# A two-layer graph network on one core: the second layer's first product from quarters, a norm in its input's place, and channel sums turned by VectorE

## The chip, the cores and the metric

The kernel runs on one core of a Trainium2 chip. A core has five engines that run side by side and wait for each other through semaphores: TensorE (PE in the profile) for matrix products, VectorE (DVE), ScalarE (ACT), GpSimd (POOL) and SyncE (SP), which here only starts transfers. The engines work on SBUF, an on-chip memory of 128 partitions; matrix products land in PSUM, a smaller memory in banks of 512 floats a partition. Each engine carries out its instructions strictly in the order in which the program lists them. The metric is the time of one execution on the device in microseconds.

## The reference

Sixteen graphs share one weighted adjacency matrix `adj` of 1024 nodes; every node carries 256 channels. All is in 32-bit floats. Two layers follow each other, each with a residual connection:

```python
h = relu(layernorm(x))
# layer 1, for each graph: attention whose queries come from a reweighted graph
c   = mean over channels of h                       # one number per node
A   = 2 * abs(abs(sigmoid(c_j - c_i) - 0.5) - 0.5)  # node by node
q   = relu((h^T @ (adj * A)) * para)^T
k,v = split(h @ kv_w)
x   = x + softmax(q k^T * scale) v                  # 4 heads of 64 channels
h = relu(layernorm(x))
# layer 2: aggregation over the normalised graph, and two linear layers
agg = A_hat @ h                                     # A_hat from adj + I and its degrees
y   = agg @ W1^T + b1                               # 256 -> 512 channels
out = relu(batchnorm(y)) @ W2^T + b2                # 512 -> 256 channels
x   = x + batchnorm(out)
```

The batch norms take their mean and variance over all nodes of all 16 graphs, so y is kept in memory (HBM) until all graphs are through, and read again.

## The kernel before

**The frame.** `attention` walks over all graphs in steps. A graph has four units (two head pairs by two halves of the queries) of four steps, 16 steps a graph. A step issues the scores of two blocks of keys (`scores`, L933), their exponentials p on ACT (L941), the running sum `acc` of p on VectorE (L962, L965) and the product with v of the step before (`Unit.values`, L976). After a unit's last step follow, at fixed later steps, a fold of acc (L1011, L1012), the softmax sums (L1025 to L1039), the attention output turned by VectorE in squares of 32 (L990), stored and fetched back, and its addition to x (L1074, L1082).

Behind each step the program issues a share of other work, the "background": generators that yield a cost for each piece. `attention` takes pieces until their summed cost reaches what is due by this step; the dues follow from constants (`total`). So the order on every engine is fixed when the program is written out. A `weave` runs side generators along a main one, and `soon` puts an action behind the next piece.

**The background of graph b**, in this order: four pieces of keys of graph b+1 (`keys_values`), the queries of graph b+1 (`queries`: seven products in place of eight, from sums and differences of quarters), the values of graph b+1, along with them the norm of graph b-1 after its attention (`normed`), the aggregation of graph b-1 (`aggregate`, seven products again), along with it the first norm of graph b+2 (`summed`), and at last `hidden(b-1)`, the second layer's first product, along with which `prepare` turns h of graph b+2 by way of memory (`squares`, `gathered`) and starts the weights of its reweighted graph.

**hidden.** For each of two halves of the nodes (512 columns) and four blocks of 128 output channels, two products over the two halves of the 256 input channels are summed in one PSUM bank (`bank`, three of them in rotation); ACT adds the bias and copies the result to SBUF (L773), POOL starts its store (L774), and VectorE takes its statistics (L777). The function `product` splits each product into two of 64 output rows.

**The weights w.** `differences` stores the channel sums of a graph and reads them back as one row broadcast to all partitions, `cbc`. For each tile of w, `weigh` lets ACT take |c_j - c_i| twice (L485) and a tanh (L493), and VectorE multiplies with adj (L472). From graph 2 on the sums are stored in the order (partition, tile), so that L485 reads cbc with a step of eight floats; graphs 0 and 1 have them in node order.

**Buffers.** x of three graphs is held at a time (pool p3, tag "x"); h has two buffers (p2, tag "h") which the norms of both layers and the turned copy `sq` share; y has four.

Of the kernel before, what the change touches and what calls it, by code (L numbers as in the profile page):

```python
# [23 lines left out]
def gnn_two_layers_kernel(  # L24
# [34 lines left out]
    vec = const.tile([P, 18], F32, name="vec")  # L59
    nc.sync.dma_start(out=vec, in_=vecs)  # L60
    b1, g1, be1 = (vec[:, i * HC : (i + 1) * HC] for i in range(3))
    b2, g2, be2 = (vec[:, 3 * HC + i * CC : 3 * HC + (i + 1) * CC] for i in range(3))
# [34 lines left out]
    def layers(shifted):  # L97
# [13 lines left out]
        py = st.enter_context(tc.tile_pool(name=f"py_{kind}", bufs=4))  # L111
# [7 lines left out]

        xs, hs, hts, ats, qs, ks, vs = {}, {}, {}, {}, {}, {}, {}  # L120
        invs = {}
        csums, cbcs, weighted, weighers = {}, {}, {}, {}
# [5 lines left out]
        def soon(action):  # L128

            queue.append(action)  # L130
# [33 lines left out]
        def bank(name):  # L164
            return ps_mm.tile([P, FB], F32, tag="mm", name=name)
# [7 lines left out]
        def load_x(b):  # L173
            xs[b] = p3.tile([P, NT, C], F32, tag="x", name=f"x_{b}")
            parts = 4 if b == 0 else 2
            for part in range(parts):
                t = slice(part * NT // parts, (part + 1) * NT // parts)
                nc.sync.dma_start(
                    out=xs[b][:, t], in_=x[b].rearrange("(t p) c -> p t c", p=P)[:, t]
                )  # L180
# [108 lines left out]

        def load_later():  # L290
            later["w1"] = big.tile([P, CC, H1], F32, tag="w1", name="w1")
            nc.sync.dma_start(out=later["w1"], in_=w1_t.rearrange("(k p) j -> p k j", p=P))
            later["dbc"] = const.tile([P, N], F32, tag="dbc", name=f"dbc_{kind}")
            nc.sync.dma_start(out=dinv_d.rearrange("(t p) -> p t", p=P), in_=dinv)
            nc.sync.dma_start(
                out=later["dbc"], in_=dinv_d.rearrange("(o n) -> o n", o=1).to_broadcast([P, N])
            )

        class Norm:
# [3 lines left out]
            def __init__(self, b, first):  # L303
                tag = "a" if first else "b"
                self.src = xs[b]
                self.st6 = p1.tile([P, NT, 6], F32, tag="st6", name=f"st6_{tag}_{b}")
                self.mv = p1.tile([P, NT, 2], F32, tag="mv", name=f"mv_{tag}_{b}")
                self.sm = p2.tile([P, 3, NT], F32, tag="lnsm", name=f"lnsm_{tag}_{b}")
                self.csum = None
                if first:  # L310
                    self.csum = p2.tile([P, NT], F32, tag="csum", name=f"csum_{b}")
                    csums[b] = self.csum
                self.h = p2.tile([P, NT, C], F32, tag="h", name=f"h_{tag}_{b}")
                hs[tag, b] = self.h
# [113 lines left out]
        def differences(b):  # L428

            cbc = p1.tile([P, N], F32, tag="cbc", name=f"cbc_{b}")
            cbcs[b] = (
                cbc.rearrange("p (t q) -> p t q", t=NT)
                if b <= 1
                else cbc.rearrange("p (q t) -> p t q", t=NT)
            )
            weighers[b] = weigh(b)
            if b == 0:
                broadcast_row(cbc, columns_of(csums[b], f"c{b}"), f"c{b}")  # L440
                return
            if b == 1:
                turned = bank(f"csumt_{b}")[0:NT, 0:P]
                nc.tensor.transpose(turned, csums[b], ident)
                row = p1.tile([P, NT // 2, P], F32, tag="s1", name=f"csumr_{b}")[0:NT, 0, :]
                nc.scalar.copy(row, turned)
                nc.sync.dma_start(out=csum_d[b].rearrange("(t p) -> t p", p=P), in_=row)
            else:
                nc.sync.dma_start(out=csum_d[b].rearrange("(p t) -> p t", p=P), in_=csums[b])
            nc.sync.dma_start(  # L450
                out=cbc, in_=csum_d[b].rearrange("(o n) -> o n", o=1).to_broadcast([P, N])
            )
# [229 lines left out]
        def aggregate(b):  # L682
# [3 lines left out]
            order = (0, 2, 5, 1, 4, 6, 3)  # L686
# [35 lines left out]
            def sixth(m):  # L722
                add(c21, m, c21)
                soon(lambda: scale(c21, 0))
# [5 lines left out]
            for i, (left, after) in enumerate(  # L730
# [5 lines left out]
                    (None, fifth),  # L736
                    (a22, sixth),
                    (a12, seventh),
# [4 lines left out]
                for th in range(NP // 2):  # L743
# [7 lines left out]
                    if th == NP // 2 - 1:  # L751
                        after(made)
                    elif i == 0:
                        combine("b", b, nc.vector)
                    yield 1.71

        def hidden(b):

# [31 lines left out]
        def normed(b):  # L790
            while (b, NH - 1) not in complete:
                yield 0.1
            keep(b)
            yield from Norm(b, False).all()
            if b + 3 < B:
                load_x(b + 3)
# [15 lines left out]
        def prepare(b, products):  # L812
# [4 lines left out]
            if b == 2:  # L817
                for k in range(CC):
                    yield from weave(islice(products, 3), (0, islice(w, AHEAD // 2)))
                    yield TOP  # L820
                    transposed(b, (k,))
                    yield 1.0
                yield from products
                return
            squares(b)
            yield from weave(islice(products, 3), (0, islice(w, AHEAD // 2)))
            gathered(b, 0)
            yield from weave(islice(products, 1), (0, islice(w, 1)))
            gathered(b, 1)
            yield from weave(islice(products, 2), (0, islice(w, AHEAD // 2 - 1)))  # L830
# [4 lines left out]
        def background(b):  # L835

            if b == 0:
                differences(1)
                for k in range(CC):
# [3 lines left out]
                w, products, norm = weighers[1], keys_values(1), Norm(2, True).all()  # L843
                yield from weave(
                    islice(products, 4), (0, double(islice(w, 8))), (0, islice(norm, 4))
                )
                yield from weave(
                    plain_queries(1), (0, norm), (0, w), (5, graph()), (7, degrees())
                )
                differences(2)  # L850
                yield from islice(products, 2)
                yield from prepare(2, products)
# [3 lines left out]
            if b + 1 < B:  # L856
# [5 lines left out]
                yield next(gather)  # L862
                yield from weave(products, (0, norm))
            else:
                yield from weave(endings.pop(), (2, normed(b - 1)))
                yield next(gather)
# [225 lines left out]
        def attention():  # L1092
# [7 lines left out]
            for s in range(len(steps) + 2):  # L1100
                if s < len(steps):
                    unit, g = steps[s]
                    b = unit.at[0]
                    if s % per_graph == 0:
# [4 lines left out]
                        total += 13.7 * (0 < b < B - 2) + 27.4 * (b == B - 1) + 3.0 * (b == 0)  # L1109
# [20 lines left out]
                if before is not None:  # L1130
                    (last, g_last), prs = before
                    last.values(g_last, prs)
                    if g_last == NG - 1:
# [6 lines left out]
                        else:  # L1140
                            for e in range(2):
                                at_end.setdefault(s + e, []).append(lambda u=last, e=e: u.fold(e))
                            wait = 5 if last.by_squares and last.at[1:] == (0, 0) else 4
                            at_mid.setdefault(s + wait - 1, []).append(last.sums)
# [18 lines left out]
        with st:  # L1163
# [22 lines left out]
            else:  # L1186
# [24 lines left out]
                load_x(1)  # L1211
                load_x(2)
                run(weave(plain_queries(0), (0, weighers[0]), (5, Norm(1, True).all())))
                attention()
# [349 lines left out]
```

## Time and profile before

| | |
|---|---|
| median of 3 runs | 2489.23 us (2488.91 to 2490.34) |
| profiled execution | 2488.76 us, its span 2487.0 us |
| PE, DVE, ACT, POOL busy | 2435.7, 1882.0, 1401.7, 429.2 us |
| PE's granted clock | 0.993 of full speed |
| matmuls of hidden (`py`) | 1024 instructions, 228.4 us |
| w's activations (L485) | 256 of 1168 ns on average |
| copies of y (L773), statistics of y (L777) | 128 of 683 ns, 128 of 677 ns |
| moved by transfers | 421.42 MB, 169 GB/s on average |

How to read it: a row of the profile names the source line, engine, operation, the written and the read tile with their shapes, and the count; then the busy time in us and the mean of one in ns; then the time for which the engine stood idle just before these instructions and who ended the wait. A matmul in 32-bit floats shows as two PE instructions. Busy times of one row may overlap, since instructions are pipelined. L171 is the line of `product`, so its rows are told apart by the tiles' names: pg queries, pk keys, pv values, pa aggregation, py hidden. SPq and POOLq are the instructions that start transfers.

### The profile page before, as it was taken

The page shows a single profiled execution, that of the slowest core. Times are in us where ns is not written, and L with a number is a line of the kernel's source. Part 1 is how long each engine was busy: PE and PEld are TensorE (multiplying, and loading weights), DVE is VectorE, ACT ScalarE, POOL GpSimd, SP SyncE. Part 2 cuts the span into 40 slices and gives each one's busy share as a digit, 9 for nine tenths or more (in the row PEclk, how much of TensorE's full clock was granted, in tenths as well). Part 3 has the DMA queues.
Part 4 walks back from the last instruction along what each step waited for, and adds up shares of the span by engine and source line. Part 5 has one row for each costly group of instructions (what it writes and reads, how often), then busy time and mean ns, then how long its engine had stood idle before and what let it go on. Part 6 is the DMA issues. An engine that isn't in the chain of part 4 may idle for free. (4 is left out here: it accounts for less than half of the span.)

```text
span 2487.0 us, 35569 instructions
## 1 busy us (share of the span) xinstructions
PE 2435.7 (98%) x13403; PEld 841.2 (34%) x13403; DVE 1882.0 (76%) x2920; ACT 1401.7 (56%) x1927; POOL 429.2 (17%) x527
## 2 busy tenths in 40 slices
PE   9999999999999999999999999999999999999995
PEld 4333333333333333333333333333333332334444
DVE  5668787877778787878787787868787877767775
ACT  7775564647473746656474747465564634345544
POOL 1640101010101001011101010110101001036652
PEclk9999999999999999999999999999999999999997
DMA  4754535354545545362645445543536344355559
GB/s 150 238 173 172 170 114 199 101 199 129 197 145 178 164 159 169 116 206 84 215 126 182 145 174 169 178 153 132 191 94 210 116 140 162 132 214 220 189 199 374
DMA packets 187909, 421.42 MB, mean 169 GB/s; under 512 B 21832, under 2 KB 81744, under 8 KB 181968
## 3 DMA queue, kind: packets, MB, share of 16 engines
q1 hardware_dynamic: 158560, 311.56, 37.9%
q0 software_dynamic: 29168, 107.50, 11.6%
q8 instruction: 108, 1.77, 0.3%
q14 instruction: 73, 0.60, 0.1%
HBM read 315.63 MB, written 103.35 MB: 168 GB/s over the span
## 5 line engine op out<-in xcount | busy, mean ns | idle before, releaser
L941 ACT ACTIVATE p<-sc 128x1024 f32<-128x1024 f32 x512 | 494.9, 1019 | 617.6 <-PE sc L933 617.2
L965 DVE TENSOR_TENSOR acc<-acc,p 128x1024 f32<-128x1024 f32 x384 | 471.3, 1227 | 165.1 <-ACT p L941 143.8
L933 PE MATMUL sc<-q,k 64*64 64x512 f32 x4096 | 498.8, 602 | 6.2 <-ACT p L941 6.2
L976 PE MATMUL o<-p,v 128*64 128x512 f32 x2048 | 494.5, 604 | 0.3 <-DVE os L990 0.3
L171 PE MATMUL pg<-w,h_a 128*64 128x512 f32 x1600 | 359.8, 592 | 0.8 <-DVE w L472 0.8
L171 PE MATMUL pa<-aht,h_b 128*64 128x512 f32 x1536 | 346.0, 592 | 1.1 <-ACT h_b L342 1.0
L485 ACT ACTIVATE w<-cbc,csum 128x512 f32<-128x512 f32 x256 | 285.8, 1168 | 0.0
L933 PEld LDWEIGHTS sc<-q,k 64*64 64x64 f32 x4096 | 131.0, 132 | 347.9 <-issue 286.5
L472 DVE SCALAR_TENSOR_TENSOR w<-w,adj 128x1024 f32<-128x1024 f32 x128 | 156.9, 1225 | 95.0 <-ACT w L493 91.1
L171 PE MATMUL py<-at,w 128*64 128x512 f32 x1024 | 228.4, 592 | 0.2 <-ACT y L773 0.2
L976 PEld LDWEIGHTS o<-p,v 128*64 128x64 f32 x2048 | 124.4, 136 | 298.3 <-issue 260.3
L994 POOL DMA_DIRECT2D out_d<-os x58 | 34.2, 590 | 1070.8 <-DVE os L990 1037.5
L171 PEld LDWEIGHTS pg<-w,h_a 128*64 128x64 f32 x1600 | 114.8, 137 | 229.2 <-issue 218.8
L171 PEld LDWEIGHTS pa<-aht,h_b 128*64 128x64 f32 x1536 | 109.9, 137 | 215.3 <-issue 202.0
L773 ACT ACTIVATE y<-py,vec 128x512 f32<-128x512 f32 x128 | 87.4, 683 | 115.4 <-PE py L171 91.8
L493 ACT ACTIVATE w<-w 128x1024 f32<-128x1024 f32 x128 | 135.1, 1055 | 1.7
L774 POOL DMA_DIRECT2D y_d<-y x128 | 69.7, 545 | 371.8 <-ACT y L773 362.6
L548 DVE TENSOR_TENSOR w<-w,w 128x1024 f32<-128x1024 f32 x112 | 132.7, 1214 | 1.5
L171 PEld LDWEIGHTS py<-at,w 128*64 128x64 f32 x1024 | 74.0, 137 | 145.5 <-issue 131.5
L171 PE MATMUL pv<-kvw_f,ht 128*64 128x256 f32 x1024 | 116.1, 379 | 0.0
L171 PE MATMUL pk<-ht,kvw_f 128*64 128x512 f32 x512 | 115.2, 592 | 0.2 <-ACT ht L404 0.2
L342 ACT ACTIVATE h_b<-x,lnsm_b 128x256 f32<-128x256 f32 x128 | 69.9, 599 | 65.9 <-DVE lnsm_b L331 65.9
(169 smaller groups left out, 2665.4 us busy)
## 6 DMA issues: line engine op xcount, KB each, us to landing
aht<-aht_d SPq DMA_DIRECT2D x224, 512.0 KB, 6.4
adj<-in_adj_dram SPq DMA_DIRECT2D x128, 512.0 KB, 4.8
y_d<-y POOLq DMA_DIRECT2D x128, 256.0 KB, 3.0
yin_f<-y_d SPq DMA_DIRECT2D x32, 1024.0 KB, 6.4
para<-in_para_dram SPq DMA_DIRECT2D x64, 256.0 KB, 3.6
x_d<-x POOLq DMA_DIRECT2D x16, 1024.0 KB, 5.2
xo_f<-x_d SPq DMA_DIRECT2D x32, 512.0 KB, 8.2
out_dram<-xo_f POOLq DMA_DIRECT2D x32, 512.0 KB, 10.8
```

Of the source, the lines that this page charges most:

```text
L171: nc.tensor.matmul(dst[r], left[:, r], right, start=start, stop=stop)
L342: nc.scalar.activation(self.h[:, t, :], self.src[:, t, :], AF.Relu, bias=self.sm[:, 1, t : t + 1], scale=self.sm[:, 0, t : t + 1], accum_o ...
L472: nc.vector.scalar_tensor_tensor(w, w, 1.0, a, op0=ALU.add, op1=ALU.mult)
L485: nc.scalar.activation(w[:, t, :].rearrange("p (t q) -> p t q", q=P), cbc[:, q * NT // NH : (q + 1) * NT // NH], AF.Abs, bias=csum[:, th * ...
L493: nc.scalar.activation(made[i], made[i], AF.Tanh, scale=-0.5 / C)
L548: nc.vector.tensor_sub(block(i)[part], block(x)[part], block(y)[part])
L773: nc.scalar.activation(y, made, AF.Identity, bias=b1[:, j : j + 1])
L774: nc.gpsimd.dma_start(out=y1_d[i][:, j, :], in_=y)
L933: nc.tensor.matmul(sc[part, e, :], ks[b][k][r, m * P + c * HW : m * P + (c + 1) * HW], qs[b][k][r, f * FB : (f + 1) * FB], start=True, sto ...
L941: nc.scalar.activation(pr, sc, AF.Exp)
L965: nc.vector.tensor_add(self.acc, self.acc, pr)
L976: nc.tensor.matmul(self.o[r, :], vs[b][k][:, m, r], pr[:, e, :], start=(m == 0), stop=(m == NT - 1),)
```

## The change

Five things change together.

1. For all graphs but the last two, `hidden` works on quarters: W1 in four blocks of (128 input by 256 output channels), the aggregated h in four blocks of (128 channels by 512 nodes), and seven products of sums and differences of blocks in place of eight. Each is made for two halves c of the output block (128 rows). The sums s1 to s4 of W1 are made once, on POOL, when W1 is loaded. The steps of the other operand are made in `steps_of` on VectorE and POOL, behind the first half of the aggregation's last product, and one more on POOL at the start of `hidden`. The results are put together on VectorE, ACT and POOL. The last two graphs keep the old form, `plain_hidden`.
2. In `aggregate` the last two products change places, and `sixth` scales its result at once.
3. x of a graph is loaded early into an h buffer, where the first norm overwrites it, and a second time, after the norm of the graph before, as the residual. x has one buffer of this kind in place of three, y has six in place of four.
4. The channel sums are turned by VectorE in squares of 32 and stored in node order by four transfers; the PE transpose of graph 1's sums goes. All reads of cbc are contiguous.
5. The order of the background around this: `prepare` follows the new number of pieces, graph 2's preparation is spread more finely, its norm moves from the keys of graph 1 to the queries, the first unit of a graph adds its output one step later, and the dues fall by 1.7 a graph.

```diff
+    b1_step = vec[:, 18:20]
+    nc.gpsimd.tensor_sub(b1_step, b1[:, HC // 2 :], b1[:, : HC // 2])
...
-        def load_x(b):
-            xs[b] = p3.tile([P, NT, C], F32, tag="x", name=f"x_{b}")
+        def load_x(b, first=False):
+            if first:
+                into, pool, tag = firsts, p2, "h"
+            else:
+                into, pool, tag = xs, p1, "x"
+            into[b] = pool.tile([P, NT, C], F32, tag=tag, name=f"x_{tag}_{b}")
...
+            a11, a12, a21, a22 = w1_quarters()
+            nc.gpsimd.tensor_add(s1, a21, a22)
+            nc.gpsimd.tensor_sub(s2, s1, a11)
+            nc.gpsimd.tensor_sub(s3, a11, a21)
+            nc.gpsimd.tensor_sub(s4, a12, s2)
...
+            turned = p1.tile([P, SQ], F32, tag="csumt", name=f"csumt_{b}")
+            nc.vector.transpose(turned, wides[b])
+            for i in range(NS):
+                nc.sync.dma_start(
+                    out=csum_d[b].rearrange("(t i s) -> i t s", i=NS, s=SQ)[i],
+                    in_=turned[i * SQ : i * SQ + NT],
+                )
...
-            order = (0, 2, 5, 1, 4, 6, 3)
+            order = (0, 2, 5, 1, 4, 3, 6)
...
             def sixth(m):
                 add(c21, m, c21)
-                soon(lambda: scale(c21, 0))
+                scale(c21, 0)
...
+                    elif i == 6 and b < B - 2:
+                        steps_of(b)
                     yield 1.71
 
+        def steps_of(b):
+            b11, b12, _, b22 = at_quarters(b)
...
+            nc.vector.tensor_sub(t1, b12, b11)
+            nc.vector.tensor_sub(t2, b22, t1)
+            nc.gpsimd.tensor_sub(b12, b22, b12)
+            steps[b] = t1, t2
...
         def hidden(b):
+            if b >= B - 2:
+                yield from plain_hidden(b)
+                return
...
+            t4 = p2.tile([P, FB], F32, tag="para", name=f"at4_{b}")
+            nc.gpsimd.tensor_sub(t4, b21, t2)
...
+            def put(y, n, j):
+                i = b * NH + n
+                nc.gpsimd.dma_start(out=y1_d[i][:, j, :], in_=y)
+                soon(lambda: nc.vector.bn_stats(stats1[:, j, i, :], y))
...
+            def m1(c):
+                part = one("1", a11, c, b11)
+                nc.scalar.activation(
+                    new("11", c), part, AF.Identity, bias=b1[:, c : c + 1]
+                )
+            def m2(c):
+                y = made["11"]
+                add(y, one("2", a12, c, b21), y)
+                put(y, 0, c)
+            def m3(c):
+                y = made["12"]
+                add(y, one("3", s4, c, b22), y)
+                put(y, 1, c)
+            def m4(c):
+                y = made["21"]
+                add(y, one("4", a22, c, t4), made["sum"])
+                put(y, 0, 2 + c)
+            def m5(c):
+                nc.scalar.copy(new("22", c), one("5", s1, c, t1))
+                if c == 1:
+                    both(c)
+            def both(c):
+                nc.gpsimd.tensor_add(new("12", c), made["21"], made["22"])
+            def m6(c):
+                y = new("21", c)
+                add(y, one("6", s2, c, t2), made["11"])
+                if c == 0:
+                    both(c)
+            def m7(c):
+                part, y = one("7", s3, c, t3), made["22"]
+                nc.vector.scalar_tensor_tensor(
+                    new("sum", c), part, b1_step[:, c : c + 1], made["21"], op0=ALU.add, op1=ALU.add
+                )
+                nc.gpsimd.tensor_add(y, y, made["sum"])
+                put(y, 1, 2 + c)
+            for c, order in ((0, (m1, m5, m6, m2, m3, m7, m4)), (1, (m1, m6, m2, m5, m7, m3, m4))):
+                for each in order:
+                    each(c)
+                    yield 0.86
...
             yield from Norm(b, False).all()
-            if b + 3 < B:
-                load_x(b + 3)
+            load_x(b + 1)
...
             squares(b)
-            yield from weave(islice(products, 3), (0, islice(w, AHEAD // 2)))
+            yield from weave(islice(products, 5), (0, islice(w, 2)))
             gathered(b, 0)
-            yield from weave(islice(products, 1), (0, islice(w, 1)))
+            yield from weave(islice(products, 3), (0, islice(w, 1)))
             gathered(b, 1)
-            yield from weave(islice(products, 2), (0, islice(w, AHEAD // 2 - 1)))
+            yield from weave(islice(products, 3), (0, islice(w, AHEAD - 3)))
             yield from products
...
-                yield from weave(
-                    islice(products, 4), (0, double(islice(w, 8))), (0, islice(norm, 4))
-                )
+                yield from weave(islice(products, 4), (0, double(islice(w, 8))))
...
-                        total += 13.7 * (0 < b < B - 2) + 27.4 * (b == B - 1) + 3.0 * (b == 0)
+                        total += 12.0 * (0 < b < B - 2) + 25.7 * (b == B - 1) + 3.0 * (b == 0)
```

## The prediction

> **What bounds the kernel now.** I read the page's first two parts first: which engine is busy, and whether evenly.
>
> ```profile
> PE 2435.7 (98%) x13403; PEld 841.2 (34%) x13403; DVE 1882.0 (76%) x2920; ACT 1401.7 (56%) x1927; POOL 429.2 (17%) x527
> PE   9999999999999999999999999999999999999995
> ```
>
> TensorE (PE) is full but for the ends; VectorE (DVE) has a quarter free. Stages differ, so I took three stretches of one middle graph: the aggregation, the second layer's first product ("hidden", which the change rewrites), and the start of the next graph. The columns are stretch, length, then busy time of PE, PEld, DVE, ACT, POOL.
>
> ```profile
> 1054.00:1094.00 40.00, 40.00 (x230) 12.47 (x224) 28.13 (x54) 14.94 (x27) 3.50 (x5) 1.00 0.58 197
> 1098.40:1123.50 25.10, 25.10 (x142) 7.70 (x140) 19.39 (x26) 20.23 (x23) 4.87 (x9) 1.00 0.71 239
> 1123.50:1132.00 8.50, 8.50 (x50) 2.60 (x48) 4.75 (x6) 6.55 (x8) 0.54 (x1) 1.00 0.40 123
> ```
>
> PE has no gap in any of them, so matmuls taken away are time. In hidden DVE has 25.1 - 19.4 = 5.7 us free. The timeline of PE gives the pace:
>
> ```profile
> 1098.43 5.32 PE L171 MATMUL py<-at,w 128*64 128x512 f32 x24
> 1103.68 1.95 PE L933 MATMUL sc<-q,k 64*64 64x512 f32 x16
> 1105.56 1.94 PE L976 MATMUL o<-p,v 128*64 128x512 f32 x8
> 1107.32 5.32 PE L171 MATMUL py<-at,w 128*64 128x512 f32 x24
> ```
>
> 24 PE instructions, three of today's products (eight each), take 1103.68 - 1098.43 = 5.25 us, 0.219 us each; an attention step's own matmuls between them take 3.64 us. A quarter product sums over one half of K, four instructions, 0.875 us.
>
> Two more readings: a GpSimd (POOL) operation over a DVE one, and weights made in the two node orders (min/median/max ns; the first line is graphs 0 and 1, already in node order).
>
> ```profile
> 2227.67 2.67 DVE L1382 TENSOR_TENSOR y_f<-y_f,y_f 128x512 f32<-128x512 f32 x1
> 2227.45 2.35 POOL L1327 TENSOR_TENSOR t_f<-yin_f,yin_f 128x1024 f32<-128x1024 f32 x1
> L485 ACT ACTIVATE w<-cbc,csum x18: 704/712/736, 18.5 to 70.0; 128x512 f32<-128x512 f32 x18
> L485 ACT ACTIVATE w<-cbc,csum x212: 1212/1232/1261, 187.8 to 1962.7; 128x512 f32<-128x512 f32 x106
> ```
>
> The DVE add with both inputs in SBUF lasts 2.67 us in place of 0.69 (L727's mean for one of this size): it ends 0.5 us after the POOL operation does.
>
> **What the Trainium skill says.** "SBUF — State Buffer", section "Who interferes with whom": a DVE instruction with two SBUF inputs and a GpSimd one that reads SBUF exclude each other for a whole instruction. The pair above agrees; and DVE operations with one input in PSUM kept 0.69 us beside POOL (L1370, 690 ns). The same page, "Door 1: The DMA port swizzle", says that an access that leaves its 16-byte line is penalised: the stride of eight floats costs 1.23 us against 0.71. "Perfetto Trace Analysis", "Matmuls": independent products should rotate through PSUM banks so that evacuation overlaps. Here three banks do so; the PE row of hidden shows 0.2 us idle in all.
>
> **The change, part by part.**
>
> *Quarters.* Graphs 0 to 13 (14 of 16) make 14 quarter products in place of 16: 8 PE instructions less, 1.75 us a graph, 14 x 1.75 = 24.5 us.
>
> *What the results now cost.* ACT made 8 copies of 0.68 us a graph, now 4. DVE gets 10 additions per graph that didn't exist (five for each half of the columns), all with an input in PSUM, and two steps behind the aggregation's last quarter; its 8 statistics stay. An addition of this size is 0.69 us, but independent ones start 0.60 us apart (1013.29, 1013.89), so 10 cost 6.1 to 6.9 us. The two steps depend on each other: 1.4 us, before hidden. POOL gets six of 128x512 a graph; L1327's 2363 ns for 1024 columns and 729 ns for 256 (L1289) give 1.27 us by a straight line, 7.6 us a graph, in POOL's idle time. Behind each on POOL's queue stand stores of y (0.54 us to issue), for which nothing waits within the graph.
>
> *Does DVE fit?* The stage becomes 25.1 - 1.75 = 23.35 us, and DVE needs 19.4 + 6.4 = 25.8: it is 2.4 us short in hidden, on top of some 2.5 us by which it runs behind already (the two steps and a fold at the stage's start). The next stretch repays it (8.50 - 4.75 = 3.75 us free). What matters is whether PE meets a bank not yet emptied. I followed the queue in order through three steps. The step's time after its scores start: softmax tiles come out at 2.2 and 3.2 us, and each step puts two acc additions (1.14 us apart) ahead of the results. Step with four quarter products: DVE ends them 2.75 us into the next step. Step with five: acc to 5.0, then evacuations at 5.6, 6.9, 8.2 with statistics and one adjacency step (1.14) between; PE reuses these banks at 6.3, 7.2 and later, in time by 0.7 and 0.3 us. DVE ends 3.3 us into the last step. There: sums 0.6, acc to 6.2, the first evacuation at 6.8; PE wants this bank at 6.5. So PE stalls about 0.4 us a graph. Bounds: 0, if DVE's wait on p (2.6 us at 1107) shrinks since ACT is freer, and 1.2, if a POOL operation holds one acc or w operation up (one such costs up to 1.27). I take 0.4: 14 x 0.4 = 5.6 us back.
>
> *Order of the aggregation's last two products, sixth's scale at once.* The same instructions; the first three quarter products don't need the last result. Nothing.
>
> *Norm in place, x loaded twice.* x comes early into the h buffer, is overwritten by its own norm, and a second copy replaces the last graph's x after its norm: 14 MB more on 421 MB. Each costs SP two issues of 0.47 us. The second copy's wait (on the last relu, L178 was held there already, 67.0 us in all) stands ahead of the aht loads as before; these run five pieces ahead. It is issued at about 1052.7 and lands in 5.2 (8.3 at most) each half, by 1061; the first addition to it, now one step later, comes at about 1070. Nothing, with 9 us of cover; without it DVE would stand still for the rest.
>
> *Channel sums in squares.* Each graph gets a small DVE transpose (below 0.2 us, from the 0.19 us of small operations), four stores in place of one, and a memset on POOL. SP issues 0.3 us more each, and cbc lands some 8 us after the transpose; the first weight is made 8 us or more after. Nothing, at worst an ACT wait of 1 us. The gain: the weights' 2 activations per tile fall from 1.23 to 0.71 us, about 8 us of ACT a graph. ACT isn't the bound; it gives softmax tiles earlier.
>
> *Graph 0.* Here ACT does hold PE:
>
> ```profile
> 159.84 2.00 PE L933 MATMUL sc<-q,k 64*64 64x512 f32 x16 [2.46 <-ACT p L941]
> 166.92 1.57 PE L933 MATMUL sc<-q,k 64*64 64x512 f32 x12 [2.08 <-ACT p L941]
> ```
>
> Between the softmax tiles stand three or four of graph 2's strided activations (2.36 us a pair). These become 1.42 us a pair and are spread over more products; the transpose at 57 us (0.3 us and 0.3 idle) goes. Of 5.1 us I take 3.5 back, bounds 0 and 5.1. Norm of graph 2 moves next to the degree sums, which shifts stalls of 0.65 and 0.75 us rather than ends them.
>
> *Graph 15.* Quarters of graph 13 run here in short steps (6.2 us), so the next norm's chain comes closer to the aggregation: 1 us lost, from 0 to 3.
>
> *Sum.* -24.5 + 5.6 - 3.5 + 1.0 = -21.4 us. The profiled execution is 2488.76 us, of which 2487.0 are span; the median is 2489.23, 0.5 above. So the execution goes to 2467.4 and the median to about 2468.
>
> **Rivals.**
>
> *A, DVE keeps up fully* (18 in 100). Speaks for it: ACT is freed by 11 us a graph, and DVE's 2.6 us waits on p fall. Against: 25.8 us of work in 23.35. Without stall and with all of graph 0: -24.5 - 5.1 = 2460.
>
> *B, DVE becomes the bound in hidden and eats most of the gain* (18 in 100). The shortage of 2.4 us and one or two locks show wholly as PE waits on banks, 1.2 to 1.6 us a graph: 14 x 1.4 = 19.6, so -24.5 + 19.6 - 3.5 + 1, about 2482.
>
> *C, slower* (10 in 100): the banks' late release at the hidden stage costs more than the product saves. It decides from 1.93 us of stall a graph (the 1.75 saved and 2.5 / 14 for graphs 0 and 15). Price: the 2.4 us shortage and a full POOL lock of 1.27 us together, less the 1.3 us that the banks seem to hold by the queue above: 2.4, giving 14 x (2.4 - 1.75) - 2.5 = +6.6, 2496. Against: DVE was 4 us late at 1027 (the os transpose, whose product ended at 1023.4) and PE lost nothing.
>
> *D, the transposed h of the next graph comes late.* The second half is fetched only after the tenth quarter product; four issues of 0.45 and 4.0 us of landing against 7.5 us until its first use: cover of 1.5 to 2 us, and landings of 6.2 exist. It adds 0 to 0.5 us a graph; inside the range.
>
> **How the numbers follow.** The forecast has 54 in 100: 2468, own range 2463 to 2476. A: 2460; B: 2482; C: 2496. The range from 2457 to 2485 leaves out C and the far ends, under 2 in 10. A measurement of this kernel tells 0.2% (5 us) from no change. Faster by more: the forecast, A and most of B, 0.86; within: the rest of B and a little of C, 0.05; slower 0.09.
>
> **What would show it.** PE instructions fall by 112 for the quarters; py busy falls to about 204 us; w's activation is at 0.71 us throughout; graphs 2 to 13 repeat 1.3 to 1.5 us faster than the 133.9 of before (2083.5 - 209.5 over 14, from the seen reductions). PE waits on DVE evacuations only in the last step of a graph. ACT's busy time falls by about 150 us, DVE's rises by about 115. The forecast is wrong if PE shows waits on DVE of over 1 us a graph, on x, on cbc or on ht.

## The result, and the profile after

The median is **2481.82 us** (2480.38 to 2484.57) against 2489.80 for the kernel before on the same chips (2488.11 to 2491.16, 11 runs of each): a ratio of 0.9972, 95% interval 0.9962 to 0.9981. The profiled execution took 2482.2 us, its span 2480.3, 6.7 less than before. So the change saves 8 us where I had forecast 21.

The first part of the page after the change:

```profile
PE 2418.3 (97%) x13290; PEld 829.3 (33%) x13290; DVE 1999.8 (81%) x3103; ACT 1261.2 (51%) x1870; POOL 565.2 (23%) x632
```

PE has 113 instructions less, VectorE 117.8 us of work more, ACT 140.5 us less. These are the sizes of the prediction (112; about 115; about 150). PE still is busy for 97% of the span. Its loss is in smaller pieces, which the three stretches of the same middle graph show (stretch, length, then busy time of PE, PEld, DVE, ACT, POOL; the aggregation, hidden, the next graph's start):

```profile
1060.00:1095.00 35.00, 35.00 (x199) 10.61 (x193) 27.56 (x52) 14.28 (x26) 5.19 (x6) 1.00 0.30 99
1096.29:1120.88 24.59, 23.84 (x134) 6.86 (x132) 23.05 (x31) 14.99 (x19) 11.44 (x13) 1.00 0.80 250
1120.88:1129.78 8.90, 8.90 (x50) 2.72 (x48) 8.67 (x12) 6.79 (x10) 1.28 (x3) 1.00 0.65 209
```

Of these three stretches PE is idle in hidden alone, for 24.59 - 23.84 = 0.75 us. VectorE, with 5.7 us free there before, is now busy for all but 1.5 us, and it catches up in the stretch after (8.67 of 8.90 us busy; 4.75 of 8.50 before). The timeline of PE has two places where it stands still (in brackets the idle time ahead of the instruction and who ended it):

```profile
1105.18 1.93 PE L174 MATMUL py<-at,w 128*64 128x512 f32 x8
1107.28 1.08 PE L174 MATMUL py<-at,w1s 128*64 128x512 f32 x4 [0.17 <-DVE y_sum L866]
1108.29 1.95 PE L1056 MATMUL sc<-q,k 64*64 64x512 f32 x16
...
1112.91 1.89 PE L174 MATMUL py<-at,w1s 128*64 128x512 f32 x8
1115.37 1.08 PE L174 MATMUL py<-at,w1s 128*64 128x512 f32 x4 [0.58 <-DVE y L837]
1116.28 1.03 PE L174 MATMUL py<-at,w 128*64 128x512 f32 x4
```

The product at 1115.37 wants the PSUM bank that the addition L837 empties; the one at 1107.28 waits in the same way for the bank that L866 reads. The page's row for hidden's products with w1s (busy us, mean ns, then idle before) shows that this happens all along: the 7.5 us are 13 waits of 0.58, one in each of the 14 graphs but one, and L866 ends another 13 of 0.17. The first line is the row of `py` before the change, the others are from after it.

```profile
L171 PE MATMUL py<-at,w 128*64 128x512 f32 x1024 | 228.4, 592 | 0.2 <-ACT y L773 0.2
L174 PE MATMUL py<-at,w1s 128*64 128x512 f32 x448 | 109.5, 598 | 9.7 <-DVE y L837 7.5
L506 ACT ACTIVATE w<-cbc,csum 128x512 f32<-128x512 f32 x256 | 170.3, 716 | 4.7 <-DMA cbc<-csum_d 4.7
```

The last line is the weights' activation, 0.716 us throughout (1.17 on average before).

**Idle time understates such a wait.** Four matmul instructions last 1.03 us in the profile (the ends of matmuls are modelled there), but the next four start 0.86 us after them: consecutive ones overlap by 0.17 us. The product at 1115.37 would have started at 1112.91 + 2 x 0.86 = 1114.63. It lost 0.74 us, of which the profile calls 0.58 idle, and the four that waited took 0.91 us to the next start in place of 0.86. The same reading of the first place gives 1107.28 - (1105.18 + 1.72) = 0.38 us and 0.06 more (1.01 to the next start, against 0.95 at 1108.76 in the kernel without waits, below). Together 1.23 us a graph, for 0.75 shown.

**Where the 6.7 us come from.** From the first score matmul of each graph, after less before: graph 1 starts 2.04 us earlier, graph 2 only 0.43, graph 3 only 0.19. Graphs 3 to 13 repeat every 135.47 us in place of 135.96 (0.49 less; 11 x 0.49 = 5.4). From there to the end of the span 1.1 more are won.

The forecast, split at the same points, with -24.5 + 5.6 = -18.9 spread evenly over 14 graphs (1.35 each) and the -3.5 and +1.0 in their places:

| | forecast | measured |
|---|---|---|
| to the start of graph 3 | -3.5 - 2 x 1.35 = -6.2 | -0.2 |
| eleven middle graphs | -11 x 1.35 = -14.9 | -5.4 |
| the rest | -1.35 + 1.0 = -0.4 | -1.1 |

Two things want explaining: 0.86 us in every middle graph, and 6 us before graph 3.

### The profile page after: what moved, and what is told of

Same layout as the page of the kernel before. It is cut to its first block, busy times and chain, and to the rows that moved or that the text cites. A ratio compares the mean times of both kernels' runs of the same rounds, so it can differ in the third digit from the quotient of the medians.

```text
span 2480.3 us, 35952 instructions
## 1 busy us (share of the span) xinstructions
PE 2418.3 (97%) x13290; PEld 829.3 (33%) x13290; DVE 1999.8 (81%) x3103; ACT 1261.2 (51%) x1870; POOL 565.2 (23%) x632
## 3 DMA queue, kind: packets, MB, share of 16 engines
q8 instruction: 107, 1.75, 0.3%
## 5 line engine op out<-in xcount | busy, mean ns | idle before, releaser
L174 PE MATMUL pg<-w,x_h 128*64 128x512 f32 x1472 | 332.0, 592 | 1.9 <-DVE x_h L579 1.9
L493 DVE SCALAR_TENSOR_TENSOR w<-w,adj 128x1024 f32<-128x1024 f32 x128 | 166.2, 1306 | 31.9 <-ACT w L514 26.1
L174 PEld LDWEIGHTS pg<-w,x_h 128*64 128x64 f32 x1472 | 105.6, 137 | 212.4 <-issue 201.0
L506 ACT ACTIVATE w<-cbc,csum 128x512 f32<-128x512 f32 x256 | 170.3, 716 | 4.7 <-DMA cbc<-csum_d 4.7
L514 ACT ACTIVATE w<-w 128x1024 f32<-128x1024 f32 x128 | 135.5, 1059 | 2.5
L174 PE MATMUL py<-at,w1s 128*64 128x512 f32 x448 | 109.5, 598 | 9.7 <-DVE y L837 7.5
L174 PE MATMUL py<-at,w 128*64 128x512 f32 x464 | 113.3, 595 | 1.3 <-DVE at L727 0.7
L368 ACT ACTIVATE x_h<-x_h,lnsm_a 128x256 f32<-128x256 f32 x120 | 70.5, 593 | 74.6 <-DMA aht<-aht_d 67.1
L1085 DVE TENSOR_TENSOR acc<-p,p 128x1024 f32<-128x1024 f32 x64 | 79.2, 1237 | 31.5 <-ACT p L1064 31.5
L1428 ACT ACTIVATE yin_f<-yin_f,sm_f 128x512 f32<-128x512 f32 x128 | 93.5, 802 | 15.0 <-DMA yin_f<-y_d 14.9
```

The source lines that it names most:

```text
L174: nc.tensor.matmul(dst[r], left[:, r], right, start=start, stop=stop)
L493: nc.vector.scalar_tensor_tensor(w, w, 1.0, a, op0=ALU.add, op1=ALU.mult)
L506: nc.scalar.activation(w[:, t, :].rearrange("p (t q) -> p t q", q=P), cbc[:, q * NT // NH : (q + 1) * NT // NH], AF.Abs, bias=csum[:, th * ...
L514: nc.scalar.activation(made[i], made[i], AF.Tanh, scale=-0.5 / C)
L1085: nc.vector.tensor_add(self.acc, self.held, pr)
L1428: nc.scalar.activation(y, y, AF.Relu, bias=sh[:, j : j + 1], scale=scale[:, j : j + 1])
```

## The experiments

**Middle graphs: what makes VectorE late?** Theory 1: the additions that empty PSUM banks stand behind statistics of y in VectorE's queue, which nobody waits for. This is VectorE's timeline in hidden's second step, up to the late bank of the last (the scores of these two steps start at 1099.82 and 1108.29):

```profile
1102.83 2.55 DVE L1088 TENSOR_TENSOR acc<-acc,p 128x1024 f32<-128x1024 f32 x2
1105.29 0.68 DVE L842 TENSOR_TENSOR y<-py,y 128x512 f32<-128x512 f32 x1
1105.89 0.68 DVE L825 BATCH_NORM_STATS2 stats<-y 128x6 f32<-128x512 f32 x1
1106.49 0.73 DVE L866 SCALAR_TENSOR_TENSOR y_sum<-py,vec,y 128x512 f32<-128x512 f32 x1
1107.14 0.68 DVE L825 BATCH_NORM_STATS2 stats<-y 128x6 f32<-128x512 f32 x1
1107.74 0.67 DVE L847 TENSOR_TENSOR y<-py,y_sum 128x512 f32<-128x512 f32 x1
1108.69 0.69 DVE L825 BATCH_NORM_STATS2 stats<-y 128x6 f32<-128x512 f32 x1 [0.27 <-POOL y L869]
1109.30 1.21 DVE L493 SCALAR_TENSOR_TENSOR w<-w,adj 128x1024 f32<-128x1024 f32 x1
1110.42 0.69 DVE L825 BATCH_NORM_STATS2 stats<-y 128x6 f32<-128x512 f32 x1
...
1112.23 2.49 DVE L1088 TENSOR_TENSOR acc<-acc,p 128x1024 f32<-128x1024 f32 x2
1114.63 0.68 DVE L837 TENSOR_TENSOR y<-py,y 128x512 f32<-128x512 f32 x1
```

One statistic stands ahead of L866, and three between it and L837; one of them waits for POOL. Theory 2: the quarter products themselves run slower. Theory 3: VectorE's work is simply too much for the stage, wherever it stands (rival B).

The first kernel leaves the statistics out, so its batch norm works on constants:

```diff
+    nc.gpsimd.memset(stats1, 1.0)
-                soon(lambda: nc.vector.bn_stats(stats1[:, j, i, :], y))
```

> The changed kernel without VectorE's eight statistics per graph on the results made from quarters (the batch norm of the first 14 graphs then lacks them). Theory 1, the evacuations wait in VectorE's queue: 8 x 0.6 us leave that queue in the stage, PE no longer waits for banks, and each of 14 graphs gets back 1.26 us (0.75 us of idle shown and 0.5 us of slower pace around it): about 2464 us, period of a middle graph 134.2 us in place of 135.47. Theory 2, quarter products run slower on PE by themselves: about 2481 us and period 135.4.

The second keeps them, six pieces later, with nine y buffers in place of six:

```diff
-        py = st.enter_context(tc.tile_pool(name=f"py_{kind}", bufs=6))
+        py = st.enter_context(tc.tile_pool(name=f"py_{kind}", bufs=9))
+        def behind(n, action):
+            soon(action if n == 1 else lambda: behind(n - 1, action))
-                soon(lambda: nc.vector.bn_stats(stats1[:, j, i, :], y))
+                behind(6, lambda: nc.vector.bn_stats(stats1[:, j, i, :], y))
```

> The changed kernel with each of these statistics put six pieces later in the order instead of one (nine y buffers for it, nothing left out). Theory 1, the statistics stand ahead of evacuations that PE needs: 2464 to 2468 us, period 134.2 to 134.5. Theory 3, the sum of VectorE's work in the stage is the bound whatever its order: 2478 to 2482. Theory 4, locks between POOL and VectorE hold the evacuations: 2474 to 2480.

Measured: 2470.11 us without statistics (2463.42 to 2471.87; ratio to the kernel before 0.9918, 0.9901 to 0.9935), 2468.59 with late ones (2467.88 to 2469.15; 0.9918, 0.9901 to 0.9934). Both repeat a middle graph every 134.28 us, 1.68 less than before. In total both gained less than expected: graphs 2 to 13 give 14.3 us in each profile, of which the first two graphs and the end took 1.6 and 0.6 back. (Graphs 0 and 1 differ from those of the changed kernel by up to 4 us each; that is the second question's.) PE's timeline of the kernel with late statistics, at the place of the longer wait, then its stretch and its row:

```profile
1105.32 1.03 PE L178 MATMUL py<-at,w 128*64 128x512 f32 x4
1106.18 2.75 PE L178 MATMUL py<-at,w1s 128*64 128x512 f32 x12
1108.76 1.03 PE L178 MATMUL py<-at,w 128*64 128x512 f32 x4
1109.71 1.95 PE L1060 MATMUL sc<-q,k 64*64 64x512 f32 x16
```

```profile
1089.95:1113.36 23.41, 23.41 (x135) 7.04 (x132) 22.33 (x30) 14.87 (x19) 11.64 (x13) 1.00 0.78 259
```

```profile
L178 PE MATMUL py<-at,w1s 128*64 128x512 f32 x448 | 106.0, 592 | 0.0
```

The twelve instructions run through. Hidden lasts 23.41 us, the 23.35 that the prediction worked out for a stage without stall, while VectorE does nearly the same work in it: 30 instructions in place of 31, 22.33 us busy. Theory 2 falls (1.68 saved of 1.75 worked out) and theory 3 too: the work fits, its order did not. Theory 4 (POOL locks) falls as well: POOL's work in the stage is still there (11.64 us; 11.44 in the changed kernel), and PE waits for nothing. The additional y buffers are not what does it, since the kernel without statistics has six and the same period. Theory 1 stands.

Does the loss follow the place of the statistics step by step? Two more kernels put them two and four pieces later (`behind(2, ...)`, `behind(4, ...)`), nine buffers both.

> The changed kernel with each statistic of the quarters' results two pieces later in the order instead of one. The first wait of a middle graph (0.17 us before the fifth product of the second step, one statistic ahead of the evacuation that PE needs) should go; the second (0.58 us, in the graph's last step) stays, since all four statistics are still ahead of it. If the idle shown is all of the loss, the period falls from 135.47 by 0.17 to 135.30; if a wait also costs pace around it, as 135.47 - 134.28 = 1.19 against 0.75 of idle says, by 0.4, to about 135.05.

> The changed kernel with each of these statistics four pieces later. Two of the four that stood ahead of the last step's evacuation now stand behind it, 1.2 us against a wait of 0.58: both waits go, period 134.28 as with six pieces. If the wait comes from the acc additions ahead of it alone, the period stays near 135.

Each left one place, the last step's. PE's timeline there, two pieces later and then four:

```profile
1112.87 1.89 PE L178 MATMUL py<-at,w1s 128*64 128x512 f32 x8
1115.36 1.08 PE L178 MATMUL py<-at,w1s 128*64 128x512 f32 x4 [0.60 <-DVE y L841]
```

```profile
1110.44 1.89 PE L178 MATMUL py<-at,w1s 128*64 128x512 f32 x8
1112.60 1.08 PE L178 MATMUL py<-at,w1s 128*64 128x512 f32 x4 [0.27 <-DVE y L841]
```

| statistics | pieces later than the store | idle shown | lost by starts | period less 134.28 | median us |
|---|---|---|---|---|---|
| changed kernel | 1 | 0.75 | 1.23 | 1.19 | 2481.82 |
| | 2 | 0.60 | 0.81 | 0.83 | 2477.61 |
| | 4 | 0.27 | 0.49 | 0.50 | 2473.21 |
| | 6 | 0 | 0 | 0 | 2468.59 |

The loss by starts is read as above (two pieces: 1115.36 - 1112.87 - 1.72 = 0.77, and 0.04). It accounts for the periods, so next to the kernel with six pieces nothing else is lost in a middle graph. For two pieces, the period of 135.11 is near the 135.05 expected if a wait costs more than it shows. That four pieces would do, as I had expected, was a miss: the wait went only with six.

**The rest of the change.** The next kernel takes the old form of hidden (two full products a tile, sixteen a graph) for every graph, with the background's pieces and dues that belong to it, and leaves the rest as changed; the core of the edit:

```diff
-                    elif i == 6 and b < B - 2:
-                        steps_of(b)
-            if b >= B - 2:
+            if b >= 0:
```

> The changed kernel with the old form of the product for all graphs (eight products, old numbers of pieces and dues), all the rest of the change kept. By theory 1 the quarters bring 14 x 0.49 us in all, so without them 2481.8 + 7, about 2489 us. If the rest of the change costs time by itself: over 2492. If the rest brings the gain and the quarters nothing: 2480 to 2483.

Measured: 2492.2 us (2489.7 to 2495.73), ratio 1.0014 (1.0007 to 1.002), 3.1 us above the kernel before on the same chip (2489.12), the period 135.96 as before. So norm in place, second load of x and turned sums together cost and gain nothing in a middle graph. The profiled execution, one of the longer (span 2492.4, 5.4 above before), shows where they do: graph 3 starts 2.9 us later, graph 14 is 0.4 shorter, and from graph 15's first scores to the end it takes 3.0 us longer.

One kernel leaves the second load of x out for graphs 1 to 15, so that x + attention there starts from the x of the graph before:

```diff
-            load_x(b + 1)
+            xs[b + 1] = xs[b]
```

> The changed kernel without the second load of x for graphs 1 to 15 (their residual is then the graph before, not their own x). If the 15 MB and their place on SP's queue cost nothing, as forecast: 2480 to 2483 us, period 135.47. If they hold up the first addition to x or other transfers: 2470 to 2478.

Measured: 2483.38 us (2480.81 to 2486.62), ratio 0.9977 (0.9968 to 0.9986), the period 135.47: the load costs nothing that can be told.

And one puts the sums of graphs 2 to 15 back into the order (partition, tile), so that ACT reads cbc with the step of eight floats:

```diff
+                if b <= 1
+                else cbc.rearrange("p (q t) -> p t q", t=NT)
...
+            if b > 1:
+                nc.sync.dma_start(out=csum_d[b].rearrange("(p t) -> p t", p=P), in_=csums[b])
```

> The changed kernel with the channel sums of graphs 2 to 15 stored and read in the old order. The weights' activations take 1.23 us again, 8 us more of ScalarE a graph. Theory 1 with the queue: p comes later, VectorE waits for it ahead of the evacuations, and the loss per middle graph grows from 1.26 us to 1.5 to 2.2 (period 135.7 to 136.4). Rival, ScalarE has room and the order of the sums is worth nothing in the middle graphs: period 135.4 to 135.5.

Measured: 2487.8 us (2482.19 to 2489.89, the profiled execution being the fastest), ratio 0.9993 (0.9986 to 1.0), the period 135.76, 0.29 more; graph 14 is 0.4 us longer. What the rest of the 6.0 us between the medians is, the profile can't say, since its own execution doesn't have it. PE's timeline of it, in the second step of hidden, and VectorE's first acc additions there:

```profile
1103.17 2.23 PE L174 MATMUL py<-at,w 128*64 128x512 f32 x8
1105.57 1.08 PE L174 MATMUL py<-at,w1s 128*64 128x512 f32 x4 [0.17 <-DVE y_sum L873]
1101.11 2.55 DVE L1095 TENSOR_TENSOR acc<-acc,p 128x1024 f32<-128x1024 f32 x2 [0.21 <-ACT p L1071]
```

The eight instructions end 2.23 us after the first starts in place of 1.93: the fifth was itself late by 0.30 us, and the timeline shows no idle time for it. So with quarters, the plain reading of cbc is worth 0.29 us a graph, which I had held to be nothing (with full products it was: 135.96 with either reading). VectorE's line shows the way: the acc additions wait for a softmax tile and start 3.30 us after this step's scores (1097.81), in the changed kernel 1102.83 - 1099.82 = 3.01, without a wait; the 0.29 pass on to each evacuation behind them.

**Graphs 0 to 2.** The timeline of PE has two waits there that the kernel before did not have; first the PE lines, then what ACT, VectorE, SP and POOL did (SPq starts transfers):

```profile
152.05 3.40 PE L1056 MATMUL sc<-q,k 64*64 64x512 f32 x16 [3.71 <-ACT p L1064]
199.75 1.94 PE L174 MATMUL pg<-w,x_h 128*64 128x512 f32 x8 [1.95 <-DVE x_h L579]
148.26 1.33 ACT L506 ACTIVATE w<-cbc,csum 128x512 f32<-128x512 f32 x2 [4.70 <-DMA cbc<-csum_d]
137.02 0.20 DVE L465 STREAM_TRANSPOSE csumt<-csum 128x32 f32<-128x32 f32 x1
141.46 0.34 SPq L471 DMA_DIRECT2D cbc<-csum_d  x1
95.11 0.23 POOL L96 TENSOR_SCALAR lnsm_a<-mv_a 128x4 f32<-128x4 f32 x1 [46.18 <-DVE mv_a L346]
96.40 1.67 POOL L267 DMA_DIRECT2D au_f<-in_adj_t_dram  x2
177.64 0.37 SPq L314 DMA_DIRECT2D dinv_d<-deg  x1
188.03 0.34 SPq L315 DMA_DIRECT2D dbc_f<-dinv_d  x1
188.95 2.05 SPq L192 DMA_DIRECT2D adj<-in_adj_dram  x2
```

In the kernel before, the corresponding issues stood at:

```profile
80.92 1.69 POOL L259 DMA_DIRECT2D au_f<-in_adj_t_dram  x2
130.51 0.33 SPq L450 DMA_DIRECT2D cbc<-csum_d  x1
174.42 0.41 SPq L294 DMA_DIRECT2D dinv_d<-deg  x1
```

Two chains. The norm of graph 2 was moved back; two of its POOL operations stand ahead of `graph()`'s loads on POOL's queue, and POOL waits 46 us for them. The loads start 15.5 us late; POOL's last step of the degrees (`deg`, L97) ends at 177.6 in place of 157.6. SP, which stores its result at 177.64 (174.42 before), waits until the store has landed before it reads it back at 188.03, and the adjacency tiles stand behind that. VectorE's weights wait for them, and PE at 199.75 waits for VectorE. Second, the sums of graph 2 are now turned by VectorE, behind its work on the queries, so cbc is asked for 11 us later. ACT stands at the head of its queue with a weight that needs cbc; the softmax behind it is late.

A kernel with the norm first in the weave, and the sums twelve pieces into it:

```diff
+                def sums():
+                    differences(2)
+                    yield 0.0
-                    plain_queries(1), (0, w), (4, norm), (5, graph()), (7, degrees())
+                    plain_queries(1), (0, norm), (0, w), (5, graph()), (7, degrees()), (12, sums())
-                differences(2)
```

> The changed kernel with graph 2's first norm back at the start of graph 1's queries and its channel sums stored 12 pieces into them, not after them. Theory: the waits in graphs 0 and 1 (3.7 us before the scores at 152 us with slow scores after, 2 us at 198 us) come from this place of norm and sums, by way of POOL's queue, dinv and SP: 2481.8 less 4 to 6, so 2476 to 2478 us. Rival, ACT has too much to do there anyway: 2480 to 2482.

And one with the norm first alone, the sums where the change put them:

> The changed kernel with graph 2's first norm back at the start of graph 1's queries; its channel sums are still stored after them. Theory of two separate waits: the norm's place held POOL's queue and through dinv SP, so the wait near 198 us goes; the sums' place makes cbc late, so the wait of 3.7 us near 152 us stays: 2478 to 2480. If the norm's place makes both: 2475 as with both repairs of graph 0; if the sums' place does: 2481 to 2483.

Measured: 2475.3 us with both (ratio 0.9945, 0.9928 to 0.9961), 2477.73 with the norm alone (0.9956, 0.9939 to 0.9973), the period of a middle graph unchanged at 135.47. Graphs 0 and 1 last 110.75 and 138.80 us in the changed kernel, 107.16 and 136.63 with the norm first, 105.52 and 136.62 with both (111.90 and 137.19 before). With the norm alone the wait at 199.75 is gone and that for the softmax shrinks, but stays:

```profile
150.31 2.00 PE L1056 MATMUL sc<-q,k 64*64 64x512 f32 x16 [1.51 <-ACT p L1064]
```

In the kernels that leave the norm where the change put it, graph 1 lasted from 137.0 to 144.9 us. Those at 142.9 or more had PE wait 4.7 to 6.2 us for VectorE near 200 us, the others 3.5 at most; which transfer makes it so uneven I didn't settle. With the norm first it was 135.5 to 136.6.

The kernel with the sums in the old order tests the second chain once more: its norm is late too (POOL waits 46.17 us), but graph 2's sums are stored without VectorE's turn:

```profile
130.51 0.33 SPq L478 DMA_DIRECT2D cbc<-csum_d  x1
148.18 2.00 PE L1063 MATMUL sc<-q,k 64*64 64x512 f32 x16
```

cbc is asked for when it was before, the wait ahead of these scores is gone, and graph 0 lasts 105.80 us, though the weights' activations take 2.36 us a pair there. Graph 1, with the norm's chain, lasts 140.67.

So both chains are real. The norm's is worth about 5.8 us of graphs 0 and 1 together by these profiles. The sums' is worth 1.7 with the norm first, and 3.1 (249.55 - 246.47) with the norm late. Single profiles of the kernels with both chains left in spread from 248.9 to 252.4 us, so the sizes are rough. With both mended, the first two graphs are 7 us shorter than before the change: the 3.5 us of the prediction were there to be had, and more.

**Both remedies together**, the late statistics and the order of graph 0:

> The changed kernel with both repairs, statistics six pieces later and graph 2's norm and sums early. If the two losses stand apart from each other: 2481.8 - 13.2 - 6.5, about 2462 us, and no wait of PE on a bank in the middle graphs (period 134.28 us). If one hides in the other: 2465 to 2469.

Measured: **2460.27 us** (2460.14 to 2460.31), ratio 0.9883 (0.9867 to 0.99); period 134.28, graphs 0 and 1 105.52 and 135.45 us. It beats both kernels, and it repeats to 0.2 us where the changed kernel spreads over 4. Apart from PE, whose matmuls no longer wait, its busy times are within 2.4 us of the changed kernel's:

```profile
PE 2411.1 (98%) x13290; PEld 831.6 (34%) x13290; DVE 2002.1 (81%) x3103; ACT 1259.4 (51%) x1870; POOL 563.3 (23%) x632
```

The two gains against the changed kernel, 13.2 us alone and 6.5 alone, add to 19.7; together they give 21.6. By the profiles, part of the difference lies in graphs 0 and 1 (8.3 us shorter than with late statistics alone, where the remedy by itself gave 7.4); the rest I did not split.

## Why the prediction was right or wrong

**Right: the direction, and what the products save.** 1.75 us a graph by instruction count; 1.68 measured where no bank is late. Also right were the sizes of the moved work on each engine, the stage's length without stall (23.35; 23.41), and "nothing" for x loaded twice (15.8 MB more, not 14) and, as far as the kernel with full products tells for the parts together, for the order of the aggregation. The 133.9 us of the prediction was no period of a middle graph: its stretch takes in graph 14, which lasts 122.64 us; the period before was 135.96.

**Wrong in size: "So PE stalls about 0.4 us a graph."** One place was right: the first evacuation of the last step, wanted 6.5 us after the scores start (the products before it end by the profile at 1112.91 + 1.89 = 1114.80, and 1114.80 - 1108.29 = 6.5). The other, in the step before, I had ruled out. Two terms were off. That the stall came out at the bound of 1.2 us is luck: the bound stood for a POOL operation that holds up an acc or w operation, and none of those ahead of the late banks was held up (2.55, 1.21 and 2.49 us in VectorE's lines above).
- VectorE was half a microsecond later than I had followed it. In the step with five products I had acc done at 5.0 and evacuations at 5.6, 6.9 and 8.2 us. Measured from the scores at 1099.82, the acc additions started at 3.0 where I had VectorE free at 2.75, lasted 2.55 us and ended at 5.6; the evacuations ended at 6.2 (L842), 7.4 (y_sum) and 8.6 (L847). So the margin of 0.3 us became a wait of 0.17, and the last step's addition ended at 7.0 (1115.31) in place of 6.8. This makes 0.75 us of shown idle time out of 0.4.
- I took a late bank to cost what it is late by the modelled end of the matmuls before it. By the starts of the matmuls each wait costs about 0.23 us more than the idle time shown: 1.19 us for two waits that show 0.75.

Together that is 0.8 us over my 0.4, and 11 x 0.8 = 8.8 of the 9.5 us by which the middle graphs missed; the product's 1.68 for 1.75 is the rest.

I also wrote the statistics into the queue ("with statistics and one adjacency step (1.14) between") and did not ask whether anyone waits for them. The whole stall was made of work that could stand later.

**Wrong in a step: "Norm of graph 2 moves next to the degree sums, which shifts stalls of 0.65 and 0.75 us rather than ends them."** I looked at the engine whose stalls I had seen, and not at the two POOL operations that the norm also issues, nor at what stands behind them there. By the way of POOL, SP and VectorE they reached PE. The same holds for the turned sums' "nothing, at worst an ACT wait of 1 us": that is true of every graph but graph 0, where the transpose stands behind VectorE's work on the queries, and ACT waited 4.70 us. The 3.5 us that I "take back" in graph 0 did not come: graph 1 starts 2.04 us earlier, graph 3 only 0.19. Nor were the shorter activations shown to be what wins time there: with the strided ones, and graph 2's sums stored without the turn, graph 0 was 4.95 us shorter than in the changed kernel (105.80; 110.75). In the kernels that leave both chains in, graph 0 lasted 107.3 us at the least.

**Graph 15**: 1 us lost was forecast; from graph 14 to the end 1.1 us were won in all, 0.7 better than forecast. The kernels split this. Graph 14 is 0.4 us shorter in every kernel with plain reading of cbc and not in the one with strided reading. From graph 15's first scores to the end, the rest of the change loses 3.0 us (full products: 431.68; 428.71 before), and the quarters of graph 13 win 3.7 (428.02). So as far as this pair of profiles tells, the quarters in short steps won time where 1 us of loss was forecast; what loses the 3.0 us stays open.

**The rivals.** The time is that of B, 2482, and PE does wait on VectorE's evacuations for about B's least, 1.2 us; but its reason is not the right one. B said that VectorE's work is more than the stage holds. With late statistics VectorE is busy for 22.33 of 23.41 us and PE waits for nothing; what it could not do in the order given, it can in another. That the time agrees to a microsecond is luck too: B's sum has 3.5 us won in graph 0, where nothing was kept. A ("keeps up fully", 2460) is the time of the kernel with both remedies, and PE waits for no bank in its middle graphs; but it took the statistics' new place, not the freer ACT that A counted on. C would have needed 1.93 us of stall a graph; it got 1.19. D: the only wait of PE on ht is one of 0.24 us at the start of the program, as before. Two of the prediction's own signs of being wrong came true: by the starts of the matmuls PE loses over 1 us a graph to VectorE, and in graph 0 it waits on cbc, by way of ACT.

## What to carry to other kernels

When work moves to an in-order engine that also empties PSUM banks, don't add up its busy time alone: list what stands ahead of each evacuation, and move behind it all that nobody waits for (six pieces later was worth 13 us here, with no work taken away). When a step is moved, follow each of its instructions on each engine's queue, the small POOL ones and the stores included, and ask at the program's start as well as in its middle. Price a PE wait by the starts of the instructions around it, not by the idle time beside it.

## What the runs showed of the hardware that I had not expected

- Consecutive groups of four 32-bit matmul instructions overlap by 0.17 us in the profile (1.03 long, 0.86 apart), so a wait of up to that length shows no idle time at all, and longer ones cost about 0.23 us more than shown.
- A long wait of PE also slows the matmuls behind it, through the granted clock. After 3.71 us of idle time 16 score instructions took 3.40 us in place of 1.95; in the kernel with full products 16 instructions took 5.49 us in place of 3.60 after 5.67 us. The first line below shows the longer of these waits (the other stands above); the second gives the changed kernel's stretch from 152 to 155 us, with the granted clock as the third number from the end; the last is from the kernel with the sums in the old order:

```profile
200.70 5.49 PE L174 MATMUL pg<-w,x_h 128*64 128x512 f32 x16 [5.67 <-DVE x_h L579]
152.00:155.00 3.00, 2.95 (x16) 0.80 (x16) 2.87 (x3) 1.81 (x2) 2.37 (x3) 0.50 0.65 225
196.28 1.94 PE L174 MATMUL pg<-w,x_h 128*64 128x512 f32 x8 [3.47 <-DVE x_h L586]
```

  The clock was 0.50 in both slow stretches (in the second from 201 to 204 us) and 1.00 again from 156 and 205 us. After 3.47 us of idle time it stayed at 1.00, and eight instructions took 1.94 us, as after 1.95 us in the changed kernel. In the kernel with late statistics a wait of 3.55 us met 0.50 (152 to 154 us). So in these traces the clock halved for waits from 3.55 us on and not for those up to 3.47, and the two above cost 1.45 and 1.89 us beyond the wait itself. The mean of 0.97 from 124 to 186 us hides this.
- The Trainium skill, "SBUF — State Buffer", section "Who interferes with whom", says that a VectorE instruction with two SBUF inputs and a GpSimd one that reads SBUF exclude each other. Here the adjacency step L493, usually 1.21 us, took 1.93 at 1116.62 beside a POOL addition of y; and POOL's addition L869, 1.28 us at the median, lasted up to 2.16. The trace agrees, but neither stood ahead of a late bank in the graph shown.
